# Where the last bias is added to x, and who copies half of the last weighed context values

## The chip, the cores and the metric

The kernel runs on one core of a Trainium2 chip. The metric is the time of one execution on the device in microseconds (us); less is better. Three executions of the kernel before took 1097.67, 1102.98 and 1100.89 us, so its median is 1100.89 us. One more execution was profiled and took 1098.87 us.

## The reference

The layer is one transformer block in fp32 on `x` of 2 batches x 1024 tokens x 256 features, with a context `ctx_768` of 2 x 154 x 192: self-attention with 16 heads of 64, cross-attention to the context, and a gated feed-forward layer of inner width 1024. Each has a layer norm ahead of it and a bias and a residual sum behind it.

```python
def _layernorm(x, g, b, eps=1e-05):
    mu = jnp.mean(x, axis=-1, keepdims=True)
    var = jnp.var(x, axis=-1, keepdims=True)
    return (x - mu) * jax.lax.rsqrt(var + eps) * g + b
...
h = _layernorm(x, ln1_g, ln1_b)
x = _attention(h, h, sa_wq, sa_wk, sa_wv, sa_wo, sa_bo) + x
h = _layernorm(x, ln2_g, ln2_b)
x = _attention(h, cond_emb, ca_wq, ca_wk, ca_wv, ca_wo, ca_bo) + x
h = _layernorm(x, ln3_g, ln3_b)
p = h @ ff_w1 + ff_b1
a, gate = (p[..., :D_FF], p[..., D_FF:])
h = a * jax.nn.gelu(gate, approximate=False) @ ff_w2 + ff_b2
return h + x
```

The bias that this change is about is `ff_b2`.

## The kernel before

All of x stays on the chip, as 16 tiles of 128 tokens x 256 features (8 of each batch). The order of every engine's instructions is written out by hand: the engines take their instructions in the order in which the program issues them, and a tile framework adds the waits between engines. Three stages follow one another, with the later ones prepared beside the earlier ones: self-attention, cross-attention, and the gated layer.

The gated layer is the last loop of the function (`for k in range(2 * FU)`, lines 1273 to 1299). It runs over four blocks of 512 tokens ("pairs" 0 to 3; 0 and 1 are batch 0, 2 and 3 are batch 1) and, for each, over eight blocks of 128 inner features: 32 units, each of two half units, so that k runs from 0 to 63. A unit makes its four blocks of a and gate (256 tokens each) with seven products on TensorE in place of eight, from sums of the weights (`weight_sums`) and of the tokens (`token_sums`, four additions on GpSimd for each pair, at k = 8, 24 and 40 for the pair that comes next). The work of a unit:

- `gate_first` (even k): products into `pa`, `pb` and `pc`, a copy of `pa` on ScalarE (line 1018), sums on VectorE (1022, 1024), and the last product of the unit before (`gate_last`, with VectorE's line 1050 and GpSimd's multiplication, line 1052).
- `gate_second` (odd k): three more products, two Gelus on ScalarE (1036, 1042), sums on VectorE (1038, 1041), and GpSimd's other multiplication (line 1043).

After its unit work each k does what else is due, in this order: `cross_weigh` at k = 1 and k = 5 (the weighed context values of the last two units of cross-attention, whose transposed weights come only now), pieces of the cross-attention's output projection (`out_piece`, line 463), from k = 16 on two products with `w2` (`sum_slot`, line 1065), then `run_work`, and at the very end one entry of the list `later`.

`run_work` takes, at odd k, one step of the list `side`. From k = 7 on these are the steps of the third layer norm of batch 1 (`norm_beside("ff", 1)`), two tiles of x to a step and four kinds of work, each lagging the one before by a step: `stats` on VectorE (lines 236, 237), `deviation` on GpSimd (242, 246), `normalize` (VectorE's line 252, then two instructions of line 263 on GpSimd, which write the tile `xn_ln`), and `turn` (four transposes on TensorE, line 276, into the bank `ph_ln`, stored by ScalarE, line 291). The first `normalize` is issued at k = 11, the first `turn` at k = 13, the last one at k = 19. The step after the last appends eight additions to `later` (`add_biases("ff", 1)`): x plus `ff_b2`, one tile each, on GpSimd, line 316. The eight of batch 0 come in the same way from the norm of batch 0 a little earlier. Before the change one such addition is issued in each of k = 5 to 12 (batch 0) and k = 21 to 28 (batch 1).

The sum of the feed-forward result and x (line 1075, VectorE) must come after the bias of its tile: the first of them, of tile 0, is issued at k = 19, the next at k = 23, then one at every fourth k.

`cross_values` multiplies the context values with the transposed weights of one unit. It makes four quarters in two parts, quarters 0 and 2 in two banks of the pool `ps_o`, quarters 1 and 3 in two banks of `ps_m`, and `store` copies them to `o_ca` (line 890). `pools` is an empty dictionary until the gated layer begins, which opens its own pool of four banks in it; so its truth value says whether the gated layer has begun.

`len(CG)` is 3 and `NF` is 8.

Of the kernel before, what the change touches and what calls it, by code (L numbers as in the profile page):

```python
# [18 lines left out]
def tile_transformer_block(ctx: ExitStack, tc: tile.TileContext, a: dict, out: bass.AP):  # L19
    nc = tc.nc  # L20
# [11 lines left out]
    NT = S // P  # L32
# [7 lines left out]
    KB = 32  # L40
# [11 lines left out]
    NF = DF // P  # L52
# [45 lines left out]
    for n in names:  # L98
        k = n_of[n]
# [67 lines left out]
    for n in names[2:]:  # L167
        own = rows[row_of[n] - n_cols:row_of[n] - n_cols + n_of[n], :]
        p = HR if n in twice else P
# [152 lines left out]
    def norm_beside(kind, b):  # L322

        after = {"sa": None, "ca": "sa", "ff": "ca"}[kind]
        stats, deviation, normalize, turn = norm_pieces(kind, b)
        n = 1 if narrow(kind, b) else 2
        lag = {}  # L330
        for fns, first in ((turn, 3), (stats, 0), (deviation, 1), (normalize, 2)):
            for i, fn in enumerate(fns):
                t = i if fns is stats else 2 * i + 1
                lag.setdefault(first + t // n, []).append((fn, fns is turn))
        for k in range(NT // n + 3):
            tiles = tile_order(kind)[k * n:(k + 1) * n]
            needs = [(after, b, half, t) for half in range(NQ) for t in tiles if after]

            def step(fns=lag[k]):
                done = [fn() for fn, _ in fns]  # L340
                return next((fn for fn in done if fn), None)

            side.append((any(turns for _, turns in lag[k]), needs, step))
        if not narrow(kind, b):
            side.append((False, (), lambda: add_biases(kind, b)))
# [130 lines left out]
    def out_order(kind):  # L476

        return [t for t in tile_order("ff" if kind == "ca" else "ca") if t % 2 == 0]
# [68 lines left out]
    later = []  # L547

    def run(piece):
        done = piece()  # L550
        if done is not None:
            (adds if getattr(done, "adds", False) else stores).append(done)

    def flush(queue):
        for fn in queue:
            fn()
        queue.clear()

    def run_work(n, n_side, bank=None, n_sum=0):

        while n > 0 and work:
            n -= work[0].banks
            run(work.pop(0))
        for _ in range(min(n_side, len(side))):
            needs_bank, needs, fn = side[0]
            if needs_bank and not bank and n <= 0 or not added.issuperset(needs):
                break  # L570
            if needs_bank and not bank:
                n -= 1
            spare["bank"] = bank or mm_tile
            run(fn)
            side.pop(0)
        for i in range(min(max(n, 0) + n_sum, len(outs))):
            spare["out"] = mm_tile if i < n else sum_tile
            run(outs.pop(0))

    def out_pieces(kind, b, half, tiles):  # L580
        outs.extend(lambda t=t: out_piece(kind, b, half, t) for t in tiles)
# [120 lines left out]
    CG = [(t, min(TG, NT - t)) for t in range(0, NT, TG)]  # L702
# [144 lines left out]
    def cross_regroup(c):  # L847

        ui, n = divmod(c - len(CG) - 2, len(CG))
        if n != 0 or not 0 <= ui < NU:  # L850
            return
        for a2 in range(2):
            for a4 in range(P // KB):
                half, e = divmod(a4, 2)
                own = slice(a4 * KB, (a4 + 1) * KB)
                src = slice((2 * half + a2) * KB, (2 * half + a2 + 1) * KB)
                blocks = pTc["ring"][src, ui % 3, :2 * NM].rearrange("p (m e) j q -> p m e (j q)", e=2)
                nc.sync.dma_start(
                    out=pTc["pairs"][own, a2].rearrange("p m j q -> p m (j q)"), in_=blocks[:, :, e])

    def cross_values(ui, a2):

        b, pr = units[ui]
        v, v0 = vs["ca", b, pr // 2], pr % 2 * P
        if a2 == 0 and pr % HP == 0:
            oT["ca", b, pr // HP] = pt_.tile([P, HP, S], F32, tag="oT", name=f"o_ca{b}_{pr}")
        quarters = (a2, 2 + a2)  # L870
        po = {a4: (mm_tile if a2 else sum_tile)(f"poc_{ui}_{a4}") for a4 in quarters}
        for m in range(NM + 1):
            for a4 in quarters:
                r0 = a4 // 2 * QG
                r = slice(r0, r0 + QG)
                for j in range(2):
                    nc.tensor.matmul(  # L877
                        po[a4][j * DH:(j + 1) * DH, :NT * KB],
                        lhsT=v[r, m + a2 * (m == NM), v0 + j * DH:v0 + (j + 1) * DH],
                        rhs=pTc["pairs"][r, a2, m, j] if m < NM else  # L880
                        pTc["ring"][r, ui % 3, NB - 1, j, :],
                        start=(m == 0), stop=(m == NM),
                        tile_position=(r0, j * DH),
                    )
        dst = oT["ca", b, pr // HP][:, pr % HP, :].rearrange(
            "p (t a q) -> p t a q", a=P // KB, q=KB)

        def store():
            for a4 in quarters:
                nc.vector.tensor_copy(  # L890
                    dst[:, :, a4, :], po[a4][:, :NT * KB].rearrange("p (t q) -> p t q", q=KB)
                )

        return store

# [11 lines left out]
    def cross_drain(c):  # L907

        n = c - 2
        if 0 <= n < CA:  # L910
            cross_turn(n)

    def cross_weigh(c):

        ui, n = divmod(c - 2 * len(CG) - 1, len(CG))
        if n == 0 and 0 <= ui < NU:
            for part in range(2):
                run(lambda: cross_values(ui, part))
            flush(stores)
# [5 lines left out]
    wsum, wh, ub, psum, pools = {}, {}, {}, {}, {}  # L925
# [50 lines left out]
    def token_sums(pair):  # L976

        b, t0 = divmod(pair * 2 * BT, S)
        h = hT["ff", b]
        own = [[h[:, c, t0 + j * BT:t0 + (j + 1) * BT] for j in range(2)] for c in range(NC)]  # L980
        t = pp_.tile([P, 3, BT], F32, tag="P", name=f"hs{pair}")
        nc.gpsimd.tensor_tensor(t[:, 0, :], own[0][1], own[0][0], ALU.subtract)
        nc.gpsimd.tensor_tensor(t[:, 1, :], own[1][1], t[:, 0, :], ALU.subtract)
        nc.gpsimd.tensor_tensor(own[0][1], own[1][1], own[0][1], ALU.subtract)
        nc.gpsimd.tensor_tensor(t[:, 2, :], own[1][0], t[:, 1, :], ALU.subtract)
        wh[pair] = {
            1: own[0][0], 2: own[1][0], 3: own[1][1], 4: t[:, 2, :],
            5: t[:, 0, :], 6: t[:, 1, :], 7: own[0][1],
        }
# [92 lines left out]
    with tc.manual_schedule():  # L1082
# [193 lines left out]
        for k in range(2 * FU):  # L1276
            c = CA + k
            if k == 0:
                run_work(0, 0, n_sum=2)
            flush(adds)  # L1280
            (gate_second if k % 2 else gate_first)(k // 2)
            flush(stores)
            flush(lates)
            if k == 2 * len(CG) + 1:
                norm_beside("ff", B - 1)
            cross_drain(c)
            if k % 2:
                cross_weigh(c - 1 if k == len(CG) + 2 else c)
            cross_regroup(c)
            if k == len(CG) + 2:  # L1290
                out_pieces("ca", B - 1, NQ - 1, out_order("ca"))
            if k % (2 * NF) == NF and k < 2 * FU - 2 * NF:
                token_sums(k // (2 * NF) + 1)
            for _ in range(min(2, len(sums))):
                run(sum_slot)
            flush(stores)
            run_work(0 if k == 1 else 1 + k % 2, k % 2)
            if later:
                later.pop(0)()
        gate_last(FU - 1)  # L1300
        while sums:
# [35 lines left out]
```

## Time and profile before

| | us |
|---|---|
| median of three executions | 1100.89 |
| the profiled execution | 1098.87 |
| its span in the profile | 1097.1 |
| outside the span | 1.77 |
| TensorE busy in the span | 1076.0 |
| VectorE, ScalarE, GpSimd busy in the span | 893.2, 638.1, 730.1 |
| TensorE idle in the gated layer, 917 to 936 | 0.51 of 19 |
| 936 to 957 | 1.02 of 21 |
| 957 to 965 | 1.85 of 8 |
| 965 to 1080 | 0 of 115 |

The span is the time from the first to the last instruction in the profile; what lies outside it is start and end. A busy share is an average: what a change of a stage can bring is read from the waits in that stage. The last four rows are taken from a table of the engines' busy time by stretches of the span, in us from its start. Lines of the profile name the engine (PE is TensorE's matmul, PEld its loading of weights, DVE VectorE, ACT ScalarE, POOL GpSimd), the source line, the operation and the tiles; "granted clock" (PEclk) is the share of full speed that TensorE's clock had.

The half units lie thus in the profiled execution, by the start of their first product: k = 0 at 917.30, k = 1 at 920.32, k = 2 at 925.04, k = 6 at 940.34, k = 8 at 946.82, k = 10 at 949.84, k = 12 at 953.26, k = 14 at 960.11, k = 16 at 964.66, k = 18 at 969.85, k = 24 at 984.54 us.

### The profile page before, as it was taken

To read this page: it belongs to the slowest core of one execution; us is meant where nothing else is said; L and a number is where in the kernel's file an instruction comes from. 1 tells how busy PE (TensorE), PEld (TensorE's weight loads), DVE (VectorE), ACT (ScalarE), POOL (GpSimd) and SP (SyncE) were. 2 spreads that over 40 slices of the span, in tenths; PEclk is the share of its full clock that TensorE was granted. 3 is DMA by queue.
4 is the path that set the end of the run, shared out by engine and by line. 5 is a ranking of instruction groups with operands and counts; after the bars stand their busy time and mean duration, and the time that the engine had idled before them with its cause. 6 is when DMAs were issued, how large, how long until landed. Compare 5 with 4: busy or idle time off the path is not lost.

```text
span 1097.1 us, 44912 instructions
## 1 busy us (share of the span) xinstructions
PE 1076.0 (98%) x18388; PEld 711.9 (65%) x18388; DVE 893.2 (81%) x1301; ACT 638.1 (58%) x2057; POOL 730.1 (67%) x1552
## 2 busy tenths in 40 slices
PE   8999999999999999999999999899999999899998
PEld 6555656556766565566575666566766677688887
DVE  5888999898989998999999989978877877644442
ACT  5666766667666666666776775666555554232221
POOL 2676777777777777777776777776756785565331
PEclk9999999999999999999999999999999999999999
DMA  3222112122111011111110210136665545000000
GB/s 82 67 57 57 46 43 52 42 49 46 35 41 45 20 42 33 38 42 24 42 42 19 47 33 18 28 99 157 170 154 124 116 106 116 1 10 14 12 15 29
DMA packets 104094, 60.71 MB, mean 55 GB/s; under 512 B 32330, under 2 KB 94674, under 8 KB 103890
## 3 DMA queue, kind: packets, MB, share of 16 engines
q1 hardware_dynamic: 102514, 57.07, 21.9%
q8 instruction: 145, 2.38, 0.9%
q10 hardware_dynamic: 1376, 0.79, 0.2%
q14 instruction: 59, 0.48, 0.2%
HBM read 27.91 MB, written 2.10 MB: 27 GB/s over the span
## 4 chain that ended last, share of the span: by engine, by line
PE 72%; ACT 7%; DMA 5%; DVE 5%; POOL 5%; SPq 3%; issue 3%; DVEq 0%; POOLq 0%; ACTq 0%
PE po L535 14%; PE s L489 14%; ACT p L500 6%; PE pf L1065 5%; PE py_ca L463 5%; DMA st<-st 5%; PE py_sa L463 4%; PE pq_ca L358 4%; PE poc L877 4%; PE pb L999 4%; PE pv_sa L389 3%; PE pk_sa L358 3%; DVE st L650 3%; PE sc L798 3%; SPq L510 3%
## 5 line engine op out<-in xcount | busy, mean ns | idle before, releaser
L500 ACT ACTIVATE p<-s,st 128x512 f32<-128x512 f32 x512 | 344.8, 686 | 195.8 <-DVE st L650 183.2
L600 POOL TENSOR_SCALAR p<-p,rd,ee 128x512 f32<-128x512 f32 x512 | 385.7, 767 | 47.7 <-DVE rd L596 46.7
L650 DVE TENSOR_REDUCE st<-s 128x2 f32<-128x1024 f32 x256 | 300.7, 1215 | 23.6 <-PE s L489 11.1
L614 DVE STREAM_TRANSPOSE pT<-p 128x1024 f32<-128x1024 f32 x256 | 302.2, 1217 | 0.2 <-POOL p L600 0.2
L489 PE MATMUL s<-k_sa,q_sa 64*32 64x512 f32 x4096 | 260.2, 592 | 8.8 <-ACT p L500 7.8
L535 PE MATMUL po<-pT,v_sa 64*32 64x256 f32 x8192 | 239.1, 376 | 0.7 <-DVE pT L614 0.7
L535 PEld LDWEIGHTS po<-pT,v_sa 64*32 64x32 f32 x8192 | 173.5, 106 | 75.1 <-issue 20.3
L489 PEld LDWEIGHTS s<-k_sa,q_sa 64*32 64x32 f32 x4096 | 80.8, 106 | 114.3 <-ACT p L500 58.7
L814 ACT ACTIVATE p<-sc,neg 128x154 f32<-128x154 f32 x256 | 96.2, 405 | 84.2 <-DVE rden L822 81.0
L825 POOL TENSOR_SCALAR p<-p,rden 128x154 f32<-128x154 f32 x256 | 96.8, 398 | 59.4 <-DVE rden L822 58.9
L500 ACT ACTIVATION_READ_ACCUMULATOR p<-s,st 128x1 f32 x512 | 103.8, 203 | 0.0
L523 POOL TENSOR_TENSOR zz<-ee,st 128x8 f32<-128x8 f32 x128 | 25.9, 202 | 73.1 <-ACT ee L521 73.1
L389 PEld LDWEIGHTS pv_sa<-sa_wv,hT_ln 64*128 64x128 f32 x1024 | 58.8, 188 | 14.6 <-DMA sa_wq<-in_L_xattn_sa_wq_dram 5.0
L389 PE MATMUL pv_sa<-sa_wv,hT_ln 64*128 64x128 f32 x1024 | 62.0, 275 | 0.3 <-ACT v_sa L398 0.3
L463 PE MATMUL py_ca<-ca_wo,o_ca 128*128 128x256 f32 x256 | 60.0, 382 | 0.5 <-DVE o_ca L890 0.5
L518 POOL TENSOR_TENSOR dd<-st 128x8 f32<-128x8 f32 x128 | 25.5, 199 | 52.0 <-DMA st<-st 47.6
L463 PE MATMUL py_sa<-sa_wo,o_sa 128*128 128x256 f32 x256 | 59.7, 385 | 0.0
L463 PEld LDWEIGHTS py_sa<-sa_wo,o_sa 128*128 128x128 f32 x256 | 47.3, 190 | 17.8 <-issue 6.2
L358 PE MATMUL pq_sa<-hT_ln,sa_wq 64*32 64x512 f32 (+1 forms) x976 | 57.9, 586 | 0.0
L358 PE MATMUL pq_ca<-hT_ln,ca_wq 64*128 64x512 f32 (+1 forms) x304 | 57.8, 590 | 0.0
L803 DVE TENSOR_REDUCE neg<-sc 128x6 f32<-128x924 f32 (+1 forms) x48 | 47.8, 998 | 11.9 <-PE sc L798 11.8
L358 PE MATMUL pk_sa<-hT_ln,sa_wk 64*32 64x512 f32 x960 | 57.3, 591 | 0.0
(117 smaller groups left out, 1454.5 us busy)
## 6 DMA issues: line engine op xcount, KB each, us to landing
wf<-pT_ca SPq DMA_DIRECT2D x128, 128.0 KB, 2.4
st<-st SPq DMA_DIRECT2D x512, 1.0 KB, 1.8
v_sa<-v_sa SPq DMA_DIRECT2D x32, 256.0 KB, 3.8
sa_wq<-in_L_xattn_sa_wq_dram SPq DMA_DIRECT2D x32, 128.0 KB, 3.5
sa_wk<-in_L_xattn_sa_wk_dram SPq DMA_DIRECT2D x32, 128.0 KB, 2.9
sa_wv<-in_L_xattn_sa_wv_dram SPq DMA_DIRECT2D x32, 128.0 KB, 3.2
ca_wq<-in_L_xattn_ca_wq_dram SPq DMA_DIRECT2D x32, 128.0 KB, 3.9
wf<-in_L_xattn_ff_w_dram SPq DMA_DIRECT2D x12, 256.0 KB
```

The lines of the kernel that those rows point to most:

```text
L358: nc.tensor.matmul(pq[r][f:f + m, at:at + n], lhsT=wt[own, c, f:f + m], rhs=h[own, c, t0:t0 + n], start=(c == 0), stop=(c == NH - 1), tile ...
L389: nc.tensor.matmul(pv[r][:, i * P:(i + 1) * P], lhsT=h[own, c, i * P:(i + 1) * P], rhs=wt[own, c, :], start=(c == 0), stop=(c == NH - 1), ...
L463: nc.tensor.matmul(py[:, e * D:(e + 1) * D], lhsT=o[:, i, (t + e) * P:(t + e + 1) * P], rhs=wo[kind][:, g * HP + i, :], start=(i == 0), st ...
L489: nc.tensor.matmul(sc[a4 * KB:(a4 + 1) * KB, j, :], lhsT=q[r, c:c + KB], rhs=k[r, h * HB:(h + 1) * HB], start=True, stop=True, tile_positi ...
L500: nc.scalar.activation(pr[:, j, :], sc[:, j, :], AF.Exp, bias=st[:, 0, 0, i, j:j + 1], accum_out=st[:, 0, 1, i, j:j + 1],)
L535: nc.tensor.matmul(po[a2][d:d + KB, :QH // 2], lhsT=v[r, t, e, d:d + KB], rhs=pT[r, d // DH * NK + n, :], start=(t == 0 and e == 0), stop= ...
L600: nc.gpsimd.tensor_scalar(pr[:, j, :], pr[:, j, :], rd[:, c:c + 1], ee[:, 0, c:c + 1], op0=ALU.mult, op1=ALU.mult,)
L614: nc.vector.transpose(halves[h][:, :, c:c + KB], groups.pop(0).rearrange("p j (n k) -> p (j n) k", k=KB))
L650: nc.vector.tensor_reduce(st[:, 0, 0, i, :], sc[i], AX.X, ALU.max, negate=True)
L814: nc.scalar.activation(pr_[:, j, i, :T], sc[:, j, i * T:(i + 1) * T], AF.Exp, bias=neg[:, j, i:i + 1], accum_out=den[:, j, i:i + 1],)
L825: nc.gpsimd.tensor_scalar(pr_[:, j, i, :T], pr_[:, j, i, :T], rden[:, j, i:i + 1], 1.0, op0=ALU.mult, op1=ALU.mult,)
L1065: nc.tensor.matmul(own[:, :D], lhsT=ub[pair][j][:, f, e * P:(e + 1) * P], rhs=w2[:, f, :], start=(f == 0), stop=(f == NF - 1),)
```

## The change

Two edits. In `cross_values`, once the gated layer has begun (that is for the last two units of cross-attention, at k = 1 and k = 5), quarters 2 and 3 are copied by ScalarE; quarters 0 and 1, and all quarters of the earlier units, stay with VectorE. In the loop of the gated layer an entry of `later` is taken only for k up to 5 and from k = 17 on.

```diff
         def store():
             for a4 in quarters:
-                nc.vector.tensor_copy(
-                    dst[:, :, a4, :], po[a4][:, :NT * KB].rearrange("p (t q) -> p t q", q=KB)
-                )
+                copy = nc.scalar.copy if pools and a4 // 2 else nc.vector.tensor_copy
+                copy(dst[:, :, a4, :], po[a4][:, :NT * KB].rearrange("p (t q) -> p t q", q=KB))
...
             run_work(0 if k == 1 else 1 + k % 2, k % 2)
-            if later:
+            if later and (k <= len(CG) + 2 or k > 2 * NF):
                 later.pop(0)()
```

In the order of instructions of the two built programs, nothing else moves. TensorE's and SyncE's orders are the same. Four copies go from VectorE to ScalarE. On GpSimd seven additions of batch 0 go from k = 6 to 12 to k = 17 to 23, and the eight of batch 1 therefore from k = 21 to 28 to k = 24 to 31; k = 21 to 23 issue an addition each in both programs, so four additions are new at k = 17 to 20 and three at k = 29 to 31.

## The prediction

> **What bounds the kernel now.** I read the page first, then TensorE's waits in the gated layer, then the chain of waits and the engines' timelines where those waits lie. The page says that TensorE is the bound nearly everywhere:
>
> ```profile
> PE 1076.0 (98%) x18388; PEld 711.9 (65%) x18388; DVE 893.2 (81%) x1301; ACT 638.1 (58%) x2057; POOL 730.1 (67%) x1552
> ```
>
> The change adds no product and removes none, so it can only win TensorE's idle time, or its slow time. Both edits act from k = 1 on, so I asked for whom TensorE waits from 900 us to the end:
>
> ```profile
> engine line waited for: us in total, times, longest us
> PE ph_ln L276 <- POOL xn_ln L263: 1.8, 1, 1.8
> PE pa L999 <- DVE o_ca L890: 0.5, 1, 0.5
> PE py_ca L463 <- DVE o_ca L890: 0.5, 1, 0.5
> PE pb L999 <- DVE own L1022: 0.4, 1, 0.4
> ```
>
> The longest wait is for the normalized x on GpSimd, the two of 0.5 us for the copies that the first edit touches, the fourth for VectorE. The chain of waits shows why `xn_ln` is late (columns: start, length, what):
>
> ```profile
> 948.45 0.73 POOL u L1052
> 949.17 0.70 POOL hs L982
> ...
> 952.04 0.68 POOL x L316
> 952.72 0.69 POOL kT L1043
> ...
> 954.47 0.69 POOL x L316
> 955.16 0.69 POOL u L1052
> 955.85 0.68 POOL x L316
> 956.53 0.68 POOL kT L1043
> ...
> 958.27 1.10 POOL xn_ln L263 x2
> 959.37 0.04 issue
> 959.41 0.90 PE ph_ln L276 x3
> ```
>
> From 948.45 to 959.4 the path is one unbroken row of GpSimd instructions, and three of them are bias additions that nobody needs yet. What TensorE loses there stands in its timeline and in the granted clock (in the last fence: the stretch, its length, the busy time of PE, PEld, DVE, ACT and POOL, then PEclk, the DMA share and GB/s):
>
> ```profile
> 956.49 0.59 PE L999 MATMUL pc<-hT_ln,w1s 128*128 128x256 f32 x2
> 958.87 1.44 PE L276 MATMUL ph_ln<-ident,xn_ln 128*128 128x128 f32 x4 [1.78 <-POOL xn_ln L263]
> 960.11 1.06 PE L999 MATMUL pa<-hT_ln,wf 128*128 128x256 f32 x2
> 960.96 1.06 PE L999 MATMUL pb<-hs,wf 128*128 128x256 f32 x2
> ```
>
> ```profile
> 960.00:961.00 1.00, 1.00 (x5) 0.82 (x4) 0.00 (x0) 0.00 (x0) 1.00 (x3) 0.50 0.00 0
> ```
>
> A pair of passes that takes 0.43 us from start to start elsewhere takes 0.85 here: the clock is at 0.50 from about 958.6 to 962.0.
>
> **The change, part by part.** *The additions of k = 6 to 12.* Those of k = 6 and 7 (942.66 and 947.02) lie ahead of idle time of GpSimd (2.95 us before 946.34, 0.70 us before 948.45), so taking them out moves nothing. Those of k = 8, 9 and 10 lie in the chain. Without them, by the start-to-start distances of the timeline: kT of k = 9 starts at 952.00 instead of 952.69 (its Gelu ended at 951.01); `rstd` of the first two tiles at 953.07; u at 953.74; kT of k = 11 wants 954.43 and waits for its Gelu (953.92 + 0.51, and 0.05 to see it) until 954.48; var +0.79, `rstd` +0.28, and `xn_ln` another +0.71: 956.26, against 958.27. So 3 x 0.687 = 2.06 less 0.05: 2.01 us earlier. VectorE's input for it (line 252 at 954.89, 0.29 long) is there.
>
> TensorE arrives at the transposes at 956.49 + 0.43 = 956.92. The first may start at 956.26 + 0.60 = 956.86 (the 0.60 is 958.87 - 958.27); the other three need the second half of `xn_ln`, which ends at 956.26 + 1.10 = 957.36, so they start at 957.40 and take 3 x 0.11. k = 14 starts at 957.73 instead of 960.11: **2.38 us**. Of this about 0.4 is the half clock in the three transposes.
>
> *The clock.* From 960.11 the first two pairs take 0.85 each and the third 0.56 instead of 0.43: 0.42 + 0.42 + 0.13 = **0.97 us** that go if the clock stays up. What stands against it staying up is that two waits for VectorE remain (below) and some 0.4 us for `xn_ln`. In the 3.4 us ahead of the drop (955.2 to 958.6) TensorE was busy 1.52 us; in 692.4 to 695.8, around a wait of 1.70 us, it was busy 1.87 and the clock stayed at 1.00. In the changed kernel the same stretch would hold about 2.6. I take the full 0.97; the low end is 0, and 0.4 less in the transposes.
>
> [...]
>
> *The next transposes*, of k = 15. TensorE reaches them at 957.73 + 7 x 0.432 = 960.75. GpSimd: u at 957.31, kT of k = 13 at 958.14 (its Gelu ends at 958.10, as before), `rstd` at 959.21, `xn_ln` at 959.90 to 961.0. The last three transposes wait 0.14 us, as they do now (964.09 to 964.66 is 0.57 where four take 0.43). So this wait keeps its size. From here GpSimd waits for Gelus that come earlier with TensorE, and the whole schedule is shifted by 964.66 - 961.32 = **3.34 us**.
>
> *What remains.* TensorE's gaps at 952.2 (0.30) and 955.96 (0.54 with its ramp) follow VectorE's line 1022, which stands behind four `stats` instructions (950.38 to 951.5, 953.81 to 954.9) in an unbroken row. No GpSimd instruction releases any of that row, so I leave them: 0.
>
> *The additions at their new place.* Four come at k = 17 to 20, each 0.69. GpSimd now idles 0.92 us before 969.80, 2.70 before 974.99, 0.96 before 976.67 and 2.78 before 980.17, so each addition hides in a gap: 0. The one at k = 17 stands behind the last `normalize`, not ahead of it, and delays u of k = 18 by today's times from 971.56 to 972.25; it is first read by the products with `w2` at k = 32. If that cover were gone, each would cost up to 0.69, 2.75 in all. ScalarE's copy at 975.73 waits 0.82 us for GpSimd now and TensorE does not notice. Line 1075 of tile 1 (k = 23, 984.74) now comes after an addition of k = 17, 12 us earlier. The three at k = 29 to 31 fall where GpSimd idles 2.77 us per unit: 0. At k = 24, with the four token sums, GpSimd's load is what it was.
>
> *The copies.* The product or projection that waits is released by the copy of quarter 1 (924.57 to 924.99, then TensorE at 925.04; 936.31, then 936.78), and that copy stays on VectorE, which sat idle 0.5 us before it. The second copy of the pair, 0.38 us on VectorE, goes beside it on ScalarE; its nearest row there is line 1018, of the same size, 0.37 us. ScalarE idles 3.05 and 6.50 us at these places, so the two Gelus and the copies of `pa` around it are not pushed. Behind the second copy TensorE has its second projection product, which would not start before 937.2 anyway, while the copy ends by 937.1 now. I take 0; the bounds are a gain of 2 x 0.38 if the framework's wait covered both copies, and a loss of 2 x 0.15 if ScalarE sees the bank later than VectorE does. Nothing is queued behind these waits on ScalarE for 0.9 us.
>
> **Sum.** 2.38 + 0.97 - 0.01 (rounding) = 3.34; the profiled execution would go from 1098.87 to 1095.5 us. The three timed runs have their median 2.02 us above the profiled one, and I expect the same of the changed kernel: 1100.89 - 3.34 = 1097.55, so **1097.5 us**. It is 0.30%, and changes within 0.5% (5.5 us) are about what a measurement of this kernel can't tell from none.
>
> **The rivals.**
> - *The stall goes, the clock does not count* (in the timed runs before the clock didn't fall, or it still falls after): 0.97 + 0.4 less, a gain of 2.0, 1098.9. For it: the drop at 958.6 and none at 693 show that the same idle time can do either.
> - *More goes than I count*: VectorE's gaps too (0.84, with 0.2 for the pair behind each), the rest of the waits for `xn_ln` (0.5) and the two for the copies (1.0). All together 3.34 + 2.5 = 5.9, so 1095.0. Against it: the copy that releases TensorE isn't moved, and VectorE's row has no gap.
> - *Nothing is won*: another step of the norm takes the place of the additions, so that `xn_ln` still starts at about 958.3; 1100.9. Against it: every GpSimd instruction from 952 on has its inputs by the times above; only one Gelu is 0.05 late.
> - *Slower*: GpSimd falls behind at k = 17 to 24, where the additions stand ahead of u and kT, so that ScalarE's copy of `pa` gets its tile late and TensorE its sums. Place: 970 to 985. Price: 4 x 0.69 = 2.75 on TensorE's path, 1.8 for a clock drop (0.8 + 0.97, as now), less the 3.34 won: +1.2, 1102.1. It decides once GpSimd's lag passes the 2.7 us that it waits for a Gelu now; my count leaves a lag of 0.7.
>
> **Chances.** Forecast 52%, no clock 20%, more 12%, nothing 11%, slower 5%. The three runs before lie 3.2 below and 2.1 above their median, so a median of a few runs can be 1 to 2 us off by itself. The range reaches from the second rival less 1.5, **1093.5**, to no change at all, **1101.0**. Faster by over 0.5% (under 1095.4) needs nearly all of the second rival, or the forecast with 2 us of luck: 20%. Slower by over 0.5% lies beyond the last rival's price and needs it with bad luck: 4%. Within 0.5%: 76%.
>
> **What would show it.** In the profile after: TensorE's wait for `xn_ln` near 957 at 0.3 to 0.5 us instead of 1.78; PEclk at 1.00 there; k = 16 starting 44.0 us after k = 0 instead of 47.36 (961.32 and 964.66 less 917.30); GpSimd's additions at k = 17 to 31 between Gelus with no wait of TensorE after 965; the waits for `o_ca` still two of 0.5 us; ScalarE's copies of line 890 at some 0.4 us. I would be wrong if `xn_ln` starts later than 957, if VectorE's gaps grow when TensorE comes sooner, or if a wait for GpSimd shows up after 965.

## The result and the profile after

| | before | after |
|---|---|---|
| median of 16 executions, us | 1099.62 | 1096.89 |
| lowest to highest | 1097.67 to 1102.98 | 1093.62 to 1098.95 |
| profiled execution, us | 1098.87 | 1095.93 |
| its span | 1097.1 | 1094.1 |
| start of k = 0 | 917.30 | 917.46 |
| start of k = 16 after k = 0 | 47.36 | 44.23 |
| k = 16 to the end of the span | 132.44 | 132.41 |

The changed kernel takes 0.9973 of the time, 95% interval 0.9963 to 0.9983: 2.7 us less. The profiles place it: the difference lies between k = 0 and k = 16, 3.13 us, while the start of k = 0 and the time from k = 16 to the end differ by 0.16 and 0.03 us. One execution, of the kernel that keeps TensorE busy (below), ran at a granted clock of 0.57 to 0.65 and took 1636 us; it is in none of the ratios. TensorE's waits from 900 us to the end, after (line, releaser, us in total, times, longest; the lines behind 890 have moved by one):

```profile
PE py_ca L463 <- DVE o_ca L891: 0.5, 1, 0.5
PE pa L998 <- DVE o_ca L891: 0.5, 1, 0.5
PE pb L998 <- DVE own L1021: 0.4, 1, 0.4
```

The wait of 1.8 us for `xn_ln` has left the list; the two for the copies and the one for VectorE stand as before. The chain of waits, after (start, length, what):

```profile
951.51 0.68 POOL hs L984
952.20 0.69 POOL kT L1042
...
953.23 0.71 POOL rstd_ln L246
953.94 0.70 POOL u L1051
954.64 0.03 issue
954.67 0.72 POOL kT L1042
...
956.44 1.10 POOL xn_ln L263 x2
957.54 0.04 issue
957.58 0.55 PE ph_ln L276 x3
```

There is no bias addition between the token sums and `xn_ln`, which starts at 956.44 instead of 958.27. TensorE's timeline at the two places where it waited, after:

```profile
957.16 0.97 PE L276 MATMUL ph_ln<-ident,xn_ln 128*128 128x128 f32 x4
957.96 0.60 PE L998 MATMUL pa<-hT_ln,wf 128*128 128x256 f32 x2
...
960.99 0.86 PE L276 MATMUL ph_ln<-ident,xn_ln 128*128 128x128 f32 x4
961.69 0.60 PE L998 MATMUL pa<-hT_ln,wf 128*128 128x256 f32 x2
```

Four transposes take 0.43 us from start to the next product when nothing holds them. Here they take 0.80 and 0.70: 0.37 and 0.27 us are still waited for the second half of `xn_ln`. A product's pair has its 0.43 us again. The granted clock, in the 3.4 us ahead of the stretch that was slow and in that stretch (length, PE busy, PEclk, DMA share, GB/s):

```profile
955.20:958.60 3.40, 2.81 (x14) 1.00 0.01 2
958.60:962.00 3.40, 3.36 (x18) 1.00 0.00 0
```

TensorE was busy for 2.81 us of the first in place of 1.52, and the clock stays at 1.00. The additions at their new place, on GpSimd's timeline from k = 17 on:

```profile
968.59 0.72 POOL L316 TENSOR_TENSOR x<-x,ff_b 128x256 f32<-128x256 f32 x1
969.27 0.72 POOL L1051 TENSOR_TENSOR u<-own 128x256 f32<-128x256 f32 x1
969.95 0.72 POOL L316 TENSOR_TENSOR x<-x,ff_b 128x256 f32<-128x256 f32 x1
972.01 0.73 POOL L1042 TENSOR_TENSOR u<-own 128x256 f32<-128x256 f32 x1 [1.33 <-ACT own L1041]
```

GpSimd still idles 1.33 us for a Gelu behind two of them. The four copies on ScalarE took 0.372 us each.

One row of the profile before was not in the prediction, and it turns out to matter: GpSimd between the first `xn_ln` and the second, before.

```profile
959.32 0.73 POOL L316 TENSOR_TENSOR x<-x,ff_b 128x256 f32<-128x256 f32 x1
960.01 0.72 POOL L1052 TENSOR_TENSOR u<-own 128x256 f32<-128x256 f32 x1
960.69 0.72 POOL L316 TENSOR_TENSOR x<-x,ff_b 128x256 f32<-128x256 f32 x1
961.37 0.73 POOL L1043 TENSOR_TENSOR kT<-own 128x256 f32<-128x256 f32 x1
...
963.13 1.09 POOL L263 TENSOR_SCALAR xn_ln<-x,rstd_ln,off_ln 128x256 f32<-128x256 f32 x2
```

GpSimd's row without a gap does not end at the first `xn_ln`: it runs on to the second, and holds five additions, not three. That gives two theories of the same 3.13 us. A, as the prediction's sum has it: three additions ahead of the first `xn_ln`, and the half clock behind the stall. B: k = 16 comes when the second `xn_ln` has come, with any clock, and the gain is five additions, 5 x 0.687 = 3.43, less the 0.3 us that GpSimd now idles for Gelus (most of it ahead of kT of k = 13, which starts at 958.41).

### The profile page after: what moved, and what is told of

It is laid out like the page before. It is cut to its first block, busy times and chain, and to the rows that moved or that the text cites. A ratio compares the mean times of both kernels' runs of the same rounds, so it can differ in the third digit from the quotient of the medians.

```text
span 1094.1 us, 44913 instructions
## 1 busy us (share of the span) xinstructions
PE 1074.5 (98%) x18388; PEld 711.6 (65%) x18388; DVE 892.2 (82%) x1297; ACT 639.2 (58%) x2061; POOL 730.1 (67%) x1552
## 3 DMA queue, kind: packets, MB, share of 16 engines
q8 instruction: 145, 2.38, 0.9%
## 4 chain that ended last, share of the span: by engine, by line
PE 70%; DVE 7%; ACT 7%; DMA 5%; POOL 4%; SPq 3%; issue 3%; DVEq 0%; POOLq 0%; ACTq 0%
PE s L489 13%; PE po L535 12%; ACT p L500 6%; PE pf L1064 5%; PE py_ca L463 5%; PE py_sa L463 4%; DVE st L650 4%; PE pq_ca L358 4%; PE poc L877 4%; DMA st<-st 4%; PE pb L998 3%; PE pv_sa L389 3%; PE sc L798 3%; PE pk_sa L358 3%; SPq L510 3%
```

## The experiments

All are told by the start of k = 16 after the start of k = 0, read from one profile of each kernel, because that distance repeats to 0.1 us (see the end); only where the clock falls on the way does it vary by some 0.3 us, as the second experiment shows. The ratio to the kernel before stands beside it.

**The second edit alone.** Copies as before, `later` as in the changed kernel.

> Only the second edit: all copies of line 890 stay on VectorE. If the additions are the whole gain and the copies nothing: k = 16 starts 44.2 us after k = 0 (before 47.36, changed kernel 44.23), the two waits for o_ca stay at 0.5 us each, ratio to the kernel before 0.997 (0.996 to 0.998). If the copies on ScalarE took part in the gain (up to 0.76 us by the prediction's bound): k = 16 at 44.5 to 45.0 us after k = 0 and a ratio of 0.998.

Measured: k = 16 at 44.24 us, the two waits for `o_ca` at 0.5 us, ratio 0.9969 (0.9955 to 0.9982). All of the gain is in the additions.

**The first edit alone.** The kernel before with

```diff
-                nc.vector.tensor_copy(
...
+                copy = nc.scalar.copy if pools and a4 // 2 else nc.vector.tensor_copy
+                copy(dst[:, :, a4, :], po[a4][:, :NT * KB].rearrange("p (t q) -> p t q", q=KB))
```

> Only the first edit: ScalarE copies quarters 2 and 3, the additions stay where they were. If the copies are worth nothing: k = 16 starts 47.4 us after k = 0, TensorE again waits some 1.8 us for xn_ln near 957, ratio 1.000 (0.999 to 1.001). If they gain what the bound allows: 46.6 us and 0.9993. The clock near 958 to 962 may fall to 0.50 as before or not; where it does not, theory A (the clock was a term of the gain) expects k = 16 some 1 us earlier, theory B (GpSimd's row up to the second xn_ln sets k = 16 whatever the clock) expects the same 47.4.

Measured: ratio 1.0002 (0.9990 to 1.0015), waits for `o_ca` unchanged; the copies are worth nothing. k = 16 came at 47.65 us, 0.3 later than in the profile of before, and the trace says why. TensorE's timeline of this run:

```profile
959.13 0.33 PE L276 MATMUL ph_ln<-ident,xn_ln 128*128 128x128 f32 x1 [1.78 <-POOL xn_ln L263]
...
961.40 1.06 PE L998 MATMUL pb<-hs,w1s 128*128 128x256 f32 x2
962.25 1.06 PE L998 MATMUL pc<-hs,w1s 128*128 128x256 f32 x2
...
964.77 0.60 PE L276 MATMUL ph_ln<-ident,xn_ln 128*128 128x128 f32 x4
```

The stall is the same 1.78 us, but the clock fell only at about 960.4, 1.5 us later than before when counted from k = 0, and so slowed products instead of transposes that waited anyway. Here TensorE, not GpSimd, was what came late to the second transposes: they took 0.43 us, without a wait. This bears out neither theory by itself; it shows that the clock's share depends on where its slow stretch lands.

**Only the three additions ahead of the first xn_ln.** The kernel before with

```diff
-            if later:
+            if later and k not in (8, 9, 10):
```

> The kernel before, but no addition at k = 8, 9 and 10, the three ahead of the first xn_ln; those of k = 11 and 12 stay, and the others move behind (k = 11 to 15). Theory A, the prediction's sum (three additions ahead of the first xn_ln, and the clock that then stays up): the full gain, k = 16 at 44.2 us after k = 0, ratio 0.997. Theory B (what sets k = 16 is the end of the second xn_ln, at the end of an unbroken row of GpSimd that holds five additions, those of k = 8 to 12; the half clock was hidden in it): first wait for xn_ln as in the changed kernel (under 0.5 us), clock 1.00, second wait near 1 us; two additions of 0.69 less 0.27 us that GpSimd idled: k = 16 at 45.3 us, ratio 0.998.

Measured: k = 16 at 45.40 us, as B says, 1.2 from A's 44.2; ratio 0.9973 (0.9958 to 0.9987). The clock stayed at 1.00. TensorE's timeline of this run:

```profile
956.12 0.27 PE L276 MATMUL ph_ln<-ident,xn_ln 128*128 128x128 f32 x1
956.55 0.55 PE L276 MATMUL ph_ln<-ident,xn_ln 128*128 128x128 f32 x3 [0.15 <-POOL xn_ln L263]
...
960.90 0.33 PE L276 MATMUL ph_ln<-ident,xn_ln 128*128 128x128 f32 x1 [0.78 <-POOL xn_ln L263]
961.44 0.55 PE L276 MATMUL ph_ln<-ident,xn_ln 128*128 128x128 f32 x3 [0.21 <-POOL xn_ln L263]
961.82 0.60 PE L999 MATMUL pa<-hT_ln,wf 128*128 128x256 f32 x2
```

At the first transposes TensorE loses what it loses in the changed kernel. For the second it is ready at 959.95 (the last product ahead starts at 959.52) and is through at 961.82: 1.87 us, of which 0.43 is work. So 1.44 us are waited, 0.27 in the changed kernel: the two additions of k = 11 and 12 are worth 1.17 us, 45.40 less 44.23, once the first stall is gone. The ratio alone could not have said so, as its interval holds both.

**Only the two between the first and the second xn_ln.** `k not in (11, 12)` in the same place.

> The kernel before, but no addition at k = 11 and 12, the two between the first and the second xn_ln. The first wait stays at 1.8 us. Theory A (only what lies ahead of the first xn_ln, and the clock, count): 47.4 us from k = 0 to k = 16, ratio 1.000. Theory B: the second xn_ln ends 1.37 us earlier; if the clock falls as before, TensorE then is what arrives late, the half clock shows, and k = 16 comes at 47.2 us; if the clock stays at 1.00, it comes at 46.2 us (two additions less the wait). Ratio 0.9988 to 1.000.

Measured: k = 16 at 47.32 us, ratio 1.0000 (0.9988 to 1.0013). The second `xn_ln` ended at 965.50, 45.56 us after k = 0 instead of 46.93, so GpSimd was 1.37 us earlier; the clock fell to 0.50 as before, TensorE reached the second transposes only at 966.82 and did them in 0.44 us without a wait. GpSimd's and TensorE's timelines of this run:

```profile
964.40 1.10 POOL L263 TENSOR_SCALAR xn_ln<-x,rstd_ln,off_ln 128x256 f32<-128x256 f32 x2
```

```profile
966.82 0.60 PE L276 MATMUL ph_ln<-ident,xn_ln 128*128 128x128 f32 x4
967.26 0.60 PE L999 MATMUL pa<-hT_ln,wf 128*128 128x256 f32 x2
```

So two bounds lay on top of each other in the kernel before: GpSimd's row (47.36) and TensorE's stall with its slow clock (47.32). Taking two additions from the one uncovers the other at once.

**TensorE kept busy in the stall.** The kernel before, and in `turn`, for the last norm of batch 1:

```diff
+            if kind == "ff" and b == B - 1 and t < 4:
+                for _ in range(14 if t == 0 else 8):
+                    nc.tensor.transpose(ph[0][:, :P], ident, ident)
```

> The kernel before with TensorE kept busy in the stall: 14 transposes of the identity into the bank ph_ln ahead of the first four transposes of batch 1's last norm and 8 ahead of the next four (0.108 us each, overwritten by the true ones). All additions stay. The clock should stay at 1.00 from 955 to 965. Theory A (the half clock is a term of the time before, 0.97 us and 0.4 in the transposes): k = 16 comes 46.0 to 46.4 us after k = 0, ratio 0.999. Theory B (the second xn_ln ends where it ends, and TensorE waits for it with any clock): 47.3 us, ratio 1.000, and a second wait for xn_ln of some 0.5 us in place of the slow clock.

The ratio is 1.0014 (0.9996 to 1.0032), no gain. The rows are those of a second profile of the same kernel:

> The same kernel as e5_keep_clock, whose profiled execution ran at a clock of 0.64 from start to end, so that its rows can't be compared. Expected as there: theory A (the half clock is a term of the time before) k = 16 at 46.0 to 46.4 us after k = 0; theory B (the second xn_ln sets k = 16) 47.3 us with the clock at 1.00 from 955 to 965 and a second wait for xn_ln of some 0.5 us.

Measured: k = 16 at 47.41 us (before 47.36). The clock and TensorE's timeline of this run (the helper's lines have moved by three):

```profile
960.50:967.50 7.00, 6.48 (x41) 1.00 0.01 2
```

```profile
960.28 1.69 PE L276 MATMUL ph_ln<-ident 128*128 128x128 f32 x14
962.24 0.33 PE L279 MATMUL ph_ln<-ident,xn_ln 128*128 128x128 f32 x1 [0.27 <-POOL xn_ln L263]
...
967.14 0.33 PE L279 MATMUL ph_ln<-ident,xn_ln 128*128 128x128 f32 x1
967.68 0.55 PE L279 MATMUL ph_ln<-ident,xn_ln 128*128 128x128 f32 x3 [0.21 <-POOL xn_ln L263]
968.06 0.60 PE L1002 MATMUL pa<-hT_ln,wf 128*128 128x256 f32 x2
```

The clock is at 1.00 in the whole stage, and k = 16 comes when it came. In the kernel before the slow clock cost nothing: without it TensorE waits for the second `xn_ln` instead, which ended at 967.62 here, 46.97 us after k = 0 (before 46.93). The timed executions agree: of 81 of the kernel before that ran beside the experiments, 17 have a mean granted clock of 1.000, so no slow stretch at all (a profile with one has 0.998), and they are no faster (mean 1101.6 us, against 1100.8 for the 46 at 0.997 or 0.998). So B has the right bound for the kernel before, but not "with any clock": as the run without the additions of k = 11 and 12 shows, TensorE's own row, stall and slow clock together, ends at the same time. The gain needs both rows to become shorter.

**All seven additions at once.** The changed kernel with

```diff
-            if later and (k <= len(CG) + 2 or k > 2 * NF):
-                later.pop(0)()
+            for _ in range(7 if k == 2 * NF + 1 else k <= len(CG) + 2 or k > 2 * NF):
+                if later:
+                    later.pop(0)()
```

> The changed kernel, but all seven held additions of batch 0 are issued at k = 17, one after another (4.8 us on GpSimd), in place of one at each of k = 17 to 23. k = 16 stays at 44.2 us after k = 0. If the late additions are hidden with some 2.7 us to spare, this row is 2.1 us beyond what GpSimd idles there, ScalarE's copy of pa at k = 20 gets its tile 2.1 us late, and TensorE's product of k = 21 is late by about 0.6: k = 22 starts 15.5 to 15.9 us after k = 16 (changed kernel 15.12). If the cover is larger: 15.1. If nothing covers it: 17 or more.

Measured: k = 16 at 44.23 us, and from k = 16 to k = 22 15.13 us (changed kernel 15.12): no cost at all. GpSimd's timeline of this run:

```profile
967.27 4.83 POOL L316 TENSOR_TENSOR x<-x,ff_b 128x256 f32<-128x256 f32 x7
972.06 0.72 POOL L1051 TENSOR_TENSOR u<-own 128x256 f32<-128x256 f32 x1
972.75 0.73 POOL L1042 TENSOR_TENSOR u<-own 128x256 f32<-128x256 f32 x1
```

The two multiplications behind the row are 4.1 and 2.1 us late (each counted from k = 0, against the changed kernel), and nobody waits: ScalarE's copy of `pa` at k = 20 started 0.69 us after its product, as it does in the changed kernel and in the one before. The expectation had read a wait for GpSimd there, because the profile before puts 0.82 us of ScalarE's idle time at this copy down to GpSimd, whose instruction came last; but the product bound it there too. The cover is larger than the prediction had it.

**What is left in the changed kernel.** Three further steps, each on top of the changed kernel, were tried for the waits that remain. First the banks:

```diff
-        po = {a4: (mm_tile if a2 else sum_tile)(f"poc_{ui}_{a4}") for a4 in quarters}
+        po = {a4: (mm_tile if a2 != bool(pools) else sum_tile)(f"poc_{ui}_{a4}") for a4 in quarters}
```

> The changed kernel, and for the last two units of cross-attention the first part takes its two banks from ps_m and the second part from ps_o, so that the banks that the next products want are copied while the second part still runs. If the two waits of 0.5 us for o_ca are waits for a bank: the one at k = 2 goes (0.5 us), the one at k = 5 shrinks to 0.1 to 0.2, because the projection still needs the copied values themselves. k = 6 then starts 22.2 us after k = 0 (changed kernel 23.04), k = 16 43.4 (44.23), if GpSimd and VectorE shift along. If GpSimd's row sets k = 16 here too: k = 6 at 22.2, k = 16 still near 44.2. Ratio to the kernel before 0.9965 or 0.997.

Measured: k = 6 at 22.09 us and k = 16 at 43.29 (changed kernel 23.04 and 44.23), ratio 0.9963 (0.9947 to 0.9980). The waits for `o_ca` were waits for a bank (at k = 5 the projection starts at 936.72, ahead of the last copies at 936.83 and 936.89; some 0.2 us of that wait stay, as expected), and GpSimd's row shifts along, since its first instruction follows VectorE's line 1049, which waits for TensorE.

Then the order within a step of the last norm, `normalize` ahead of `deviation`:

```diff
-        for fns, first in ((turn, 3), (stats, 0), (deviation, 1), (normalize, 2)):
+        plan = ((turn, 3), (stats, 0), (deviation, 1), (normalize, 2))
+        if kind == "ff" and b == B - 1:
+            plan = plan[:2] + plan[:1:-1]
+        for fns, first in plan:
```

> The changed kernel, and in the last norm of batch 1 a step issues normalize ahead of deviation, so that xn_ln no longer stands behind the next tiles' var and rstd (0.97 us on GpSimd). What is left of TensorE's waits for xn_ln in the changed kernel (0.37 and 0.27 us) goes: k = 16 at 43.6 us after k = 0, ratio to the kernel before 0.9965. If VectorE's line 252 then sets xn_ln: the first wait shrinks only in part, 43.8 to 44.0.

Measured: k = 16 at 43.88 us, 0.35 won where 0.64 was waited; ratio 0.9972 (0.9957 to 0.9986). Both waits for `xn_ln` are gone (the transposes take 0.44 us), but TensorE, sooner at k = 15, then loses 0.17 us to VectorE's line 1024, which is 1021 in the changed kernel, and the first pair behind that wait takes 0.54 us in place of 0.43.

Both steps together:

> The changed kernel with the swapped banks and normalize first. If the two gains lie one after the other: k = 16 at 42.7 to 42.8 us after k = 0 and a ratio to the kernel before of 0.9957 (0.9945 to 0.997). If VectorE's row of statistics takes over as the bound of k = 8 to 14, 43.2 or more.

Measured: k = 16 at 42.93 us, ratio 0.9963 (0.9945 to 0.9980). The two gains add up (0.94 and 0.35). Only one wait of TensorE is left in the list, for VectorE's line 1024, 0.4 us. So VectorE's row was taken apart: of the two statistics of a step the second is issued half a unit later.

```diff
+            parts = [lag[k]]
+            if kind == "ff" and b == B - 1:
+                i = 1 + any(turns for _, turns in lag[k])
+                own = [lag[k].pop(i)] if k * n < NT else []
+                parts.append(own)
...
-            run_work(0 if k == 1 else 1 + k % 2, k % 2)
+            run_work(0 if k == 1 else 1 + k % 2, 1 if k > 2 * len(CG) else k % 2)
```

> The kernel of e8_both, with the second of the two statistics of each step issued half a unit later, at even k, so that VectorE's row of four stats instructions ahead of lines 1050 and 1022 becomes two and two. If that row is what TensorE waits for in k = 9 to 15 (0.30, 0.55 and 0.17 us with their ramps): those waits go, GpSimd's row leaves a wait of 0.1 to 0.3 for xn_ln, and k = 16 comes 41.9 to 42.2 us after k = 0 (e8_both 42.93). If GpSimd's row takes over whole: 42.6 or more. Ratio to the kernel before 0.995 (0.9935 to 0.9965).

Measured: k = 16 at 42.07 us, as expected; ratio 0.9945 (0.9928 to 0.9963), against 0.9973 (0.9963 to 0.9983) of the change itself. TensorE's list of longer waits from 900 us on holds one, and that lies ahead of k = 0 (in its timeline a gap of 0.27 us is left ahead of 956.17):

```profile
PE poc L886 <- DVE pT_ca L850: 0.2, 1, 0.2
```

By k = 16 it is 2.16 us ahead of the changed kernel. The intervals of the two ratios only just meet, and each was taken against its own runs of the kernel before; that it is faster than the changed kernel rests on the distance in the traces.

## Why the prediction was right, and where it was not

- *The forecast.* 1097.5 us and faster by 3.34 us were said; 1096.89 and 2.73 us (ratio 0.9973) were measured, 3.13 us between k = 0 and k = 16. The median of before, with more runs, lies 1.27 us below the one the prediction started from, and the gain was 0.61 us smaller; that these two partly cancel in the time is luck. The distance is not: 44.0 us was said for k = 16 after k = 0, 44.23 measured.
- *The first xn_ln.* 956.26 was said, which is 956.42 in a profile whose k = 0 starts 0.16 later; 956.44 was measured. k = 14 came 2.31 us earlier, for 2.38: the three transposes that wait for the second half of `xn_ln` began 0.02 us later than said and took 0.38 us in place of 3 x 0.11.
- *The clock.* It stayed at 1.00, and the way from k = 14 to the second transposes shrank from 3.98 to 3.03 us, for the 0.97 that was said. As an account of the gain this is one half: the sum follows TensorE's row alone. "Those of k = 8, 9 and 10 lie in the chain" stopped GpSimd's row at the first `xn_ln`, but it goes on to the second, with the additions of k = 11 and 12, and with these two in place the clock at 1.00 brings k = 16 only to 45.40 us. The working for the second transposes did leave the two out of GpSimd's times, so the sum came out right; it did not name them or price them. Behind the first stall they are worth 1.17 us (45.40 less 44.23). Taken alone from the kernel before, neither side counts: 47.41 us with the clock kept up, 47.32 without the two additions, against 47.36. What a fallen clock would cost with all five additions out, no run shows: it stayed up in every one.
- *The rival "no clock", 2.0 us.* It did not come, since the clock stayed up. Its price did not hold for the kernel before either: with the clock up and the additions in place nothing is won. The slow clock shows in the time only where GpSimd's row doesn't cover it: by 0.3 us in the run with the copies alone, where it came later, and in the run without the additions of k = 11 and 12, where GpSimd was 1.37 us earlier and k = 16 was not.
- *The second wait.* 0.14 us was said to stay; 0.27 is there. kT of k = 13 started at 958.41, 0.11 later than said, behind a Gelu that came 0.07 late: VectorE's line 252 took 0.37 us in place of 0.29 and pushed line 1021, and TensorE's product at 956.19 with it. These 0.13 and the 0.07 of k = 14 make up 3.34 - 3.13, but for rounding.
- *VectorE's gaps, the copies.* The gap ahead of VectorE's line 1022 did not quite stay: it grew from 0.37 to 0.45 us, which is one of the signs of being wrong that the prediction named, and is behind the late Gelu above. The two waits for `o_ca` stayed at 0.5 us. The copies' price of 0 was measured as 1.0002 (0.9990 to 1.0015) and, from the other side, as 44.24 against 44.23; ScalarE began each copy 0.05 to 0.06 us after VectorE's, where the bound had assumed 0.15.
- *The additions at their new place.* 0, as said. The point from which the rival "slower" would decide was put at a lag of 2.7 us of GpSimd; a lag of 4.1 us cost nothing, and where the point lies no run shows.

## What to carry to other kernels

When an engine's row has no gap, follow it past the first instruction that somebody waits for, to the last one that somebody waits for: what is taken out anywhere ahead of that counts, and the slack that seems to appear in between, a slow clock included, can be covered by the row itself. Where two rows end at the same time, a run that shortens one of them alone shows no gain, whichever it is; so what a part is worth is read with the others already gone, as the 1.17 us were here. And work that nobody needs soon belongs behind the stage in which its engine has no gap; here it cost nothing there, because the later stage idles.

## What the runs showed of the hardware

The granted clock fell in a wait of TensorE, or up to 1.3 us behind its end, that was much shorter than the slow stretch that followed. Three profiles have the stall of 1.78 to 1.79 us ahead of k = 14 and a stretch of about 3.4 us at half clock by it: the kernel before from 958.6 to 962.0, the first edit alone from 960.4 to 963.8, the run without the additions of k = 11 and 12 from 961.5 to 964.9, which is 41.3, 42.9 and 41.5 us after k = 0. The eight profiles in which the changes had removed that stall, and the second profile of the kernel in which TensorE was kept busy in it, have a PEclk of 1.00 from 955 to 966. Five of these nine, with a mean granted clock of 0.998, as the kernel before has it with its one slow stretch, had it fall somewhere outside those 11 us.

At another wait of nearly that length it did not fall: near 693 us, where TensorE waits for ScalarE in self-attention (1.70 us before 693.68 in the kernel before, 1.64 before 694.02 in the changed one), PEclk is 1.00 from 688 to 700 in both profiles. In the 3.4 us ahead of the three falls TensorE was busy 1.52, some 1.4 and some 1.3 us. The prediction set beside the first of these the 1.87 us of 692.4 to 695.8, where the clock stayed up; but 691.7 to 695.1, as long a stretch around the same wait, holds 1.46 us, and the clock was at 1.00 there too. So these rows do not bear out the prediction's comparison, and what made the clock fall at one wait and not at the other, no run shows.

The spread of the times of one kernel, some 5 us, does not come from the gated layer, as far as one profile of each kernel shows. In the twelve profiles (the two kernels and ten experiments) k = 16 to the end of the span took 132.38 to 132.46 us, while k = 0, ahead of which all these kernels are the same, started anywhere from 916.1 to 922.4 us. So a distance within one stage told 0.1 us apart, or 0.3 where the clock falls in it, where medians of a dozen executions left an interval of some 3 us.
